# Four algebraic changes to a four-layer graph network on one core: one gate sum for two gates, layer 3 as P + adj²R, the softmax division inside a norm, layer 1's diagonal multiplied in when a transpose is copied out

## The chip, the cores and the metric

The kernel runs on one core of a Trainium2 chip. The metric is the device time of one execution in microseconds (us). All arithmetic is fp32. The runs of one kernel agree within 0.3%.

The engines are named as in the profile: PE is TensorE (matmul), PEld its weight load, DVE is VectorE, ACT is ScalarE, POOL is GpSimd.

## The reference, cut to what matters

The input x has 64 samples of 256 tokens with 128 features, adj is 256x256. Each of the four layers is `x = layernorm(x + layer(x))`. Cuts are marked `...`.

```python
# layer 0, five steps
m  = einsum('nm,bmd->bnd', adj, h)              # m_in == m_out, so av = [m, m]
u3 = h @ u3_w.T + u3_b
z  = sigmoid(av @ w3_w.T + w3_b + u3)
r  = sigmoid(av @ w4_w.T + w4_b + u3)           # the same u3 in both gates
hv = tanh(av @ w5_w.T + w5_b + (r * h @ u5_w.T + u5_b))
h  = (1 - z) * h + z * hv
# layer 1: A is a softmax over edges, built from adj and e alone
out = (A * I) @ (x @ W0) + (A * (1 - I)) @ (x @ W1) + bias
# layer 2
h = x @ Wp + bp
scores = leaky(s_src[:, :, None] + s_dst[:, None, :])      # slope 0.2
scores = where(adj <= 0, lowest, scores)
attn   = softmax(scores)
h_gat  = relu(layernorm((attn * adj) @ h) * gat_g + gat_b)
h_gin  = (1 + eps) * h_gat + adj @ h_gat
z      = relu(layernorm(h_gin @ W1 + b1) * mlp_g + mlp_b)
out    = relu(z @ W2 + b2 + h_gat)
# layer 3: both adjacency inputs are adj
out = x V0 + adj x (V1+V4) + adj^2 x (V2+V5) + adj^3 x (V3+V6)
```

## The kernel before, in the parts that matter

A pair is two samples, that is four tiles of 128 tokens; there are 32 pairs. Layer 0 treats four pairs together, in eight groups of five steps (40 steps), with features on partitions.

```python
# layer 0, one step of a group of four pairs
for i, p in enumerate(pairs):                   # adj times h: four 256-column matmuls into one bank per pair
    ...
for i, p in enumerate(pairs):
    for g, store in ((1, r), (0, z)):
        t = ps()                                # a PSUM bank, 8 in all
        nc.tensor.matmul(t, mat("u3"), hT[p], start=True, stop=False)
        nc.tensor.matmul(t, w345[:, g, :], mT[p], start=False, stop=True)
        ...
        nc.scalar.activation(store[p], t, AF.Sigmoid, bias=bzrh[:, g:g + 1])
    nc.vector.tensor_mul(r[p], r[p], hT[p])
for i, p in enumerate(pairs):                   # candidate hv and new h: two matmuls, tanh, three VectorE operations
    ...
for i, p in enumerate(pairs):                   # h back to tokens on partitions
    t = ps()
    for c in range(4):
        nc.tensor.transpose(t[:, c * P:(c + 1) * P], hT[p][:, c * P:(c + 1) * P], ident)
    ...                                         # VectorE copies it out

# a norm: VectorE, then POOL, then VectorE again
for t in range(4): nc.vector.bn_stats(st[:, t, :], y[:, t, :])
for t in range(4): nc.vector.bn_aggr(mv[:, t, :], st[:, t, :])
nc.gpsimd.tensor_scalar(rs, mv[:, :, 1], LN_EPS, None, op0=ALU.add)
nc.gpsimd.tensor_tensor(rs, rs, neg_half, op=ALU.pow)
for t in range(4): nc.vector.tensor_scalar(o[:, t, :], y[:, t, :], mv[...], rs[...], ...)

# layer 2, attention (l2_scores), its norm's gain and bias (l2_gat)
for c in range(4): nc.vector.scalar_tensor_tensor(u[:, c, :], sd[...], h[:, c, D:D + 1], maskb[...], ...)
nc.vector.scalar_tensor_tensor(l, u, 0.2, u, op0=ALU.mult, op1=ALU.max)         # leaky
nc.vector.tensor_reduce(nm, l, AX.X, ALU.max, negate=True)
for c in range(4): nc.scalar.activation(u[:, c, :], l[:, c, :], AF.Exp, bias=nm[...], accum_out=rd[...])
nc.vector.reciprocal(rd, rd)
for c in range(4): nc.vector.scalar_tensor_tensor(l[:, c, :], u[...], rd[...], a[...], op0=mult, op1=mult)
...
nc.gpsimd.tensor_mul(hg, hg, row("gat_g", 4))
nc.gpsimd.tensor_add(hg, hg, row("gat_b", 4))
nc.vector.tensor_scalar(hg, hg, 0.0, None, op0=ALU.max)                         # "the relu" below
nc.gpsimd.tensor_add(hb, hg, row("b2", 4))                                      # "hb" below

# layers 1 to 3: one stage of each of twelve pairs per tick
stages = [l1_mix, l1_out, l2_xT, l2_scores, l2_wT, l2_gat, l2_gin, l2_z, l2_zT, l2_out, l3_powers, l3_out]
for tick in range(NPAIR + len(stages) - 1):
    for s in reversed(range(len(stages))):
        if 0 <= tick - s < NPAIR:
            stages[s](tick - s)
```

Of the kernel before, what the change touches and what calls it, by code (L numbers as in the profile page):

```python
# [7 lines left out]
F32 = mybir.dt.float32  # L8
# [22 lines left out]
def kernel(ctx: ExitStack, tc: tile.TileContext, x, adj, adjT, mats, cols, rows, out):  # L31
# [60 lines left out]

    w345 = const.tile([P, 3, D], F32, name="w345")
    for i, w in enumerate(("w3", "w4", "w5")):
        nc.vector.tensor_add(w345[:, i, :], mat(w + "a"), mat(w + "b"))
    bzrh = const.tile([P, 3], F32, name="bzrh")
    nc.vector.tensor_add(bzrh[:, 0:1], col("w3_b"), col("u3_b"))
    nc.vector.tensor_add(bzrh[:, 1:2], col("w4_b"), col("u3_b"))
    nc.vector.tensor_add(bzrh[:, 2:3], col("w5_b"), col("u5_b"))

# [1 line left out]
    def ln_stats(y):  # L102
        st = small.tile([P, 4, 6], F32, tag="st", name="st")
        mv = small.tile([P, 4, 2], F32, tag="mv", name="mv")
        for t in range(4):
            nc.vector.bn_stats(st[:, t, :], y[:, t, :])  # L106
        for t in range(4):
            nc.vector.bn_aggr(mv[:, t, :], st[:, t, :])  # L108
        rs = small.tile([P, 4], F32, tag="rs", name="rs")
        nc.gpsimd.tensor_scalar(rs, mv[:, :, 1], LN_EPS, None, op0=ALU.add)  # L110
        nc.gpsimd.tensor_tensor(rs, rs, neg_half, op=ALU.pow)  # L111
        return mv, rs
# [14 lines left out]
    def layer0(pairs):  # L127
# [8 lines left out]
        for s in range(STEPS):  # L136
            for i, p in enumerate(pairs):
                t = ps()
                for b in range(2):
                    for j in range(2):  # L140
                        nc.tensor.matmul(t[:, b * N:(b + 1) * N], h[p][:, 2 * b + j, :], aT[:, j, :],  # L141
                                         start=(j == 0), stop=(j == 1))
                mT[p] = gates.tile([P, 2 * N], F32, tag=f"mT{i}", name="mT", bufs=1)
                nc.scalar.copy(mT[p], t)  # L144
            for i, p in enumerate(pairs):
                for g, store in ((1, r), (0, z)):
                    t = ps()
                    nc.tensor.matmul(t, mat("u3"), hT[p], start=True, stop=False)  # L148
                    nc.tensor.matmul(t, w345[:, g, :], mT[p], start=False, stop=True)  # L149
                    store[p] = gates.tile([P, 2 * N], F32, tag=f"g{g}{i}", name="gate", bufs=1)  # L150
                    nc.scalar.activation(store[p], t, AF.Sigmoid, bias=bzrh[:, g:g + 1])  # L151
                nc.vector.tensor_mul(r[p], r[p], hT[p])  # L152
            hv = {}
            for i, p in enumerate(pairs):
                t = ps()
                nc.tensor.matmul(t, w345[:, 2, :], mT[p], start=True, stop=False)  # L156
                nc.tensor.matmul(t, mat("u5"), r[p], start=False, stop=True)  # L157
                hv[p] = gates.tile([P, 2 * N], F32, tag=f"hv{i}", name="hv", bufs=1)
                nc.scalar.activation(hv[p], t, AF.Tanh, bias=bzrh[:, 2:3])  # L159
                nc.vector.tensor_sub(hv[p], hv[p], hT[p])  # L160
                nc.vector.tensor_mul(hv[p], hv[p], z[p])  # L161
                new = gates.tile([P, 2 * N], F32, tag=f"hT{i}", name="hT")
                nc.vector.tensor_add(new, hT[p], hv[p])  # L163
                hT[p] = new
            for i, p in enumerate(pairs):
                t = ps()
                for c in range(4):
                    nc.tensor.transpose(t[:, c * P:(c + 1) * P], hT[p][:, c * P:(c + 1) * P], ident)  # L168
                if s < STEPS - 1:
                    h[p] = gates.tile([P, 4, D], F32, tag=f"htok{i}", name="h", bufs=1)  # L170
                    nc.vector.tensor_copy(h[p], as_tiles(t))
                else:
                    y = gates.tile([P, 4, D], F32, tag="y", name="y", bufs=3)
                    nc.vector.tensor_add(y, as_tiles(t), x_sb[p])
                    layer_norm(y, x_sb[p])
# [28 lines left out]
    # the number of each edge, -1 elsewhere; rowk marks the row that edge k lies in  # L204
# [32 lines left out]
    # from edge 255 on, the index stops at the last entry  # L237
# [11 lines left out]
    dg = const.tile([P, 2, P], F32, name="dg")  # L249
    for it in range(2):  # L250
# [3 lines left out]
        nc.vector.tensor_sub(blk, blk, dg[:, it, :])  # L254
    offT = const.tile([P, 2, N], F32, name="offT")
# [37 lines left out]
    pw = const.tile([P, 2, 3, N], F32, name="pw")  # L293
    nc.vector.tensor_copy(pw[:, :, 0, :], aT)
    for k in (1, 2):
        t = ps()
        for jt in range(2):
            for kt in range(2):
                nc.tensor.matmul(t[:, jt * N:(jt + 1) * N], a[:, kt, jt * P:(jt + 1) * P], pw[:, kt, k - 1, :],
                                 start=(kt == 0), stop=(kt == 1))  # L300
        nc.vector.tensor_copy(pw[:, :, k, :], t.rearrange("p (t i) -> p t i", i=N))
    v = const.tile([P, 3, D], F32, name="v")
    for k in range(3):
        nc.vector.tensor_add(v[:, k, :], mat(f"v{k + 1}"), mat(f"v{k + 4}"))
# [7 lines left out]
    live = {}  # L312

    def l1_mix(p):
# [6 lines left out]
        for c in range(4):  # L321
            nc.tensor.matmul(d[:, c * P:(c + 1) * P], xs[:, c, :], dg[:, c % 2, :], start=True, stop=True)
# [3 lines left out]
        nc.scalar.copy(dT, d)  # L326
# [23 lines left out]
    def l2_scores(p):  # L350
# [14 lines left out]
        l = work.tile([P, 4, N], F32, tag="l", name="l")  # L365
        for c in range(4):
            b, it = divmod(c, 2)
            nc.vector.scalar_tensor_tensor(u[:, c, :], sd[:, b * N:(b + 1) * N], h[:, c, D:D + 1], maskb[:, it, :],
                                           op0=ALU.add, op1=ALU.add)
        nc.vector.scalar_tensor_tensor(l, u, 0.2, u, op0=ALU.mult, op1=ALU.max)  # L370
        nm = small.tile([P, 4], F32, tag="nm", name="nm")
        nc.vector.tensor_reduce(nm, l, AX.X, ALU.max, negate=True)
        rd = small.tile([P, 4], F32, tag="rd", name="rd")
        for c in range(4):
            nc.scalar.activation(u[:, c, :], l[:, c, :], AF.Exp, bias=nm[:, c:c + 1], accum_out=rd[:, c:c + 1])
        nc.vector.reciprocal(rd, rd)
        for c in range(4):
            nc.vector.scalar_tensor_tensor(l[:, c, :], u[:, c, :], rd[:, c:c + 1], a[:, c % 2, :],  # L378
                                           op0=ALU.mult, op1=ALU.mult)
        live["w", p] = l  # L380
        live["h", p] = h

    def l2_wT(p):
        w = live.pop(("w", p))
        wT = work.tile([P, 2, 2, N], F32, tag="wT", name="wT")
        for b in range(2):
# [5 lines left out]
            nc.scalar.copy(wT[:, b], t.rearrange("p (t i) -> p t i", i=N))  # L392
        live["wT", p] = wT

    def l2_gat(p):
# [8 lines left out]
        mv, rs = ln_stats(tt)  # L404
# [53 lines left out]
    def l3_powers(p):  # L458
        xk = work.tile([P, 2, 4, N], F32, tag="xk", name="xk")
        for b in range(2):  # L460
            lo, hi = ps(), ps()
            xs = [x_sb[p][:, 2 * b + j, :] for j in range(2)]
            for j in range(2):
                nc.tensor.transpose(lo[:, j * P:(j + 1) * P], xs[j], ident)
            for j in range(2):
                nc.tensor.matmul(lo[:, N:], xs[j], pw[:, j, 0, :], start=(j == 0), stop=(j == 1))
            for j in range(2):
                nc.tensor.matmul(hi, xs[j], pw[:, j, 1:3, :].rearrange("p k i -> p (k i)"),  # L468
                                 start=(j == 0), stop=(j == 1))
            nc.scalar.copy(xk[:, b, 0:2, :], lo.rearrange("p (k i) -> p k i", i=N))  # L470
            nc.vector.tensor_copy(xk[:, b, 2:4, :], hi.rearrange("p (k i) -> p k i", i=N))  # L471
        live["xk", p] = xk

    def l3_out(p):
        xk = live.pop(("xk", p))
        t = ps()
        for c in range(4):
            b, i = divmod(c, 2)
            for k in range(4):
                nc.tensor.matmul(t[:, c * D:(c + 1) * D], xk[:, b, k, i * P:(i + 1) * P],  # L480
                                 v[:, k - 1, :] if k else mat("v0"), start=(k == 0), stop=(k == 3))
        y = work.tile([P, 4, D], F32, tag="y", name="y", bufs=3)
        nc.vector.tensor_add(y, as_tiles(t), x_sb[p])
# [4 lines left out]
    stages = [l1_mix, l1_out, l2_xT, l2_scores, l2_wT, l2_gat, l2_gin, l2_z, l2_zT, l2_out, l3_powers, l3_out]  # L488
# [44 lines left out]
```

## Time and profile before

| | before |
|---|---|
| time, median of 4 runs | 2407.32 us (2406.32 to 2408.09) |
| span of the profiled execution | 2405.4 us |
| layer 0 and preparation, to the first matmul of layer 1's mix | 1435.3 us |
| layers 1 to 3, from there | 970.1 us |
| one step of layer 0 (40 of them) | 34.07 us |
| one full tick of layers 1 to 3 | 29.56 us |

The page of a profile gives sums and averages over the span. How the kernel is bound can only be read from a stage of its own: one step of layer 0, and one tick. A timeline line has its start, its length, the engine, the source line, the operation, the tiles, and in brackets the engine's idle time before it and what ended it.

The prediction shows the lines for the bound. Two more of the same tick of before matter later: what POOL and VectorE did to each other around the relu, in the timeline of all engines.

```profile
1861.52 1.27 POOL L328 TENSOR_TENSOR xb<-x,rbc 128x512 f32<-128x512 f32 x1
...
1861.60 1.47 DVE L412 TENSOR_SCALAR hg<-hg 128x512 f32<-128x512 f32 x1 [1.77 <-POOL hg L411]
...
1862.99 1.21 DVE L370 SCALAR_TENSOR_TENSOR l<-u 128x1024 f32<-128x1024 f32 x1
...
1863.15 2.18 POOL L414 TENSOR_TENSOR hb<-hg,rbc 128x512 f32<-128x512 f32 x1 [0.36 <-DVE hg L412]
```

The relu began just after a POOL sum (xb, which is x plus layer 1's bias) and took 1.47 us, where its best is 0.41. Then the roles change: VectorE began the leaky operation, whose inputs are both in SBUF, and the POOL sum that came just after it took 2.18 us in place of 1.27. Whoever comes second waits.

### The profile page before, as it was taken

To read this page: it belongs to the slowest core of one execution; us is meant where nothing else is said; L and a number is where in the kernel's file an instruction comes from. 1 tells how busy PE (TensorE), PEld (TensorE's weight loads), DVE (VectorE), ACT (ScalarE), POOL (GpSimd) and SP (SyncE) were. 2 spreads that over 40 slices of the span, in tenths; PEclk is the share of its full clock that TensorE was granted. 3 is DMA by queue.
4 is the path that set the end of the run, shared out by engine and by line. 5 is a ranking of instruction groups with operands and counts; after the bars stand their busy time and mean duration, and the time that the engine had idled before them with its cause. 6 is when DMAs were issued, how large, how long until landed. Compare 5 with 4: busy or idle time off the path is not lost.

```text
span 2405.4 us, 24775 instructions
## 1 busy us (share of the span) xinstructions
PE 2072.7 (86%) x8820; PEld 1407.6 (59%) x8820; DVE 1327.4 (55%) x3770; ACT 700.5 (29%) x1321; POOL 431.2 (18%) x519
## 2 busy tenths in 40 slices
PE   7996999998998998998999996888888888888887
PEld 4554555554555555555555555776666667666665
DVE  3435444335345335435444446777777777777766
ACT  2331333223322332332233323332222222222221
POOL 0000000000000000000000003444444444443342
PEclk9997999999999999999999998999999999999999
DMA  6000000000000000000000000000000000000000
GB/s 178 1 1 0 0 1 0 1 0 0 1 0 0 1 0 1 1 0 1 0 1 0 0 1 1 1 5 10 9 10 9 10 10 10 10 10 9 14 13 24
DMA packets 35035, 20.66 MB, mean 9 GB/s; under 512 B 1248, under 2 KB 34528, under 8 KB 34912
## 3 DMA queue, kind: packets, MB, share of 16 engines
q1 hardware_dynamic: 34064, 17.04, 2.7%
q10 hardware_dynamic: 848, 2.04, 0.2%
q8 instruction: 70, 1.15, 0.2%
q14 instruction: 53, 0.43, 0.1%
HBM read 10.69 MB, written 8.39 MB: 8 GB/s over the span
## 4 chain that ended last, share of the span: by engine, by line
PE 41%; DVE 40%; POOL 13%; issue 3%; ACT 3%; DMA 0%; POOLq 0%; ACTq 0%; DVEq 0%
PE ps L148 11%; PE ps L149 11%; PE ps L141 11%; POOL rs L111 8%; DVE st L106 5%; DVE hv L161 5%; DVE hv L160 4%; DVE hT L163 4%; DVE x L117 4%; DVE mv L108 2%; DVE l L378 2%; POOL hg L411 2%; POOL rs L110 2%; POOL hg L410 2%; DVE hg L412 2%
## 5 line engine op out<-in xcount | busy, mean ns | idle before, releaser
L152 DVE TENSOR_TENSOR gate<-gate,hT 128x512 f32<-128x512 f32 x160 | 110.8, 692 | 656.5 <-ACT gate L151 656.5
L110 POOL TENSOR_SCALAR rs<-mv 128x4 f32<-128x4 f32 x192 | 44.0, 229 | 1855.3 <-DVE mv L108 1853.0
L148 PE MATMUL ps<-hT,W 128*128 128x512 f32 x640 | 327.2, 593 | 9.8 <-DVE hT L134 9.8
L149 PE MATMUL ps<-mT,w 128*128 128x512 f32 x640 | 326.8, 592 | 0.0
L151 ACT ACTIVATE gate<-ps,bzrh 128x512 f32<-128x512 f32 x320 | 219.8, 687 | 342.0 <-PE ps L149 342.0
L141 PE MATMUL ps<-aT,h 128*128 128x256 f32 x1024 | 266.2, 425 | 0.0
L141 PEld LDWEIGHTS ps<-aT,h 128*128 128x128 f32 x1024 | 223.4, 222 | 36.5
L144 ACT COPY mT<-ps 128x512 f32<-128x512 f32 x160 | 93.6, 585 | 461.9 <-PE ps L141 461.9
L149 PEld LDWEIGHTS ps<-mT,w 128*128 128x128 f32 x640 | 121.6, 190 | 153.1 <-issue 153.1
L148 PEld LDWEIGHTS ps<-hT,W 128*128 128x128 f32 x640 | 121.1, 190 | 147.7 <-issue 102.1
L168 PE MATMUL ps<-ident,hT 128*128 128x128 f32 x640 | 107.6, 309 | 111.3 <-DVE hT L163 111.3
L111 POOL TENSOR_TENSOR rs<-rs,neg_half 128x4 f32<-128x4 f32 x192 | 199.2, 1038 | 15.9
L160 DVE TENSOR_TENSOR hv<-hv,hT 128x512 f32<-128x512 f32 x160 | 109.7, 686 | 109.6 <-ACT hv L159 109.6
L117 DVE TENSOR_SCALAR x<-y,mv,rs 128x128 f32<-128x128 f32 x384 | 109.5, 347 | 108.5 <-POOL rs L111 108.5
L168 PEld LDWEIGHTS ps<-ident,hT 128*128 128x128 f32 x640 | 80.5, 155 | 149.1 <-issue 149.1
L157 PE MATMUL ps<-gate,W 128*128 128x512 f32 x320 | 163.4, 592 | 0.0
L156 PE MATMUL ps<-mT,w 128*128 128x512 f32 x320 | 163.4, 592 | 0.0
L159 ACT ACTIVATE hv<-ps,bzrh 128x512 f32<-128x512 f32 x160 | 110.0, 687 | 162.8 <-PE ps L157 162.8
L409 ACT ACTIVATE hg<-ps,nmr,rs 128x128 f32<-128x128 f32 x128 | 48.1, 456 | 306.5 <-DVE nmr L406 306.5
L480 PE MATMUL ps<-v,xk 128*128 128x128 f32 x768 | 121.2, 300 | 1.5 <-DVE xk L471 1.5
L468 PE MATMUL ps<-pw,x 128*128 128x512 f32 x256 | 120.8, 594 | 1.5 <-DVE h L359 1.5
L106 DVE BATCH_NORM_STATS2 st<-y 128x6 f32<-128x128 f32 x512 | 112.8, 278 | 1.3
(157 smaller groups left out, 3169.0 us busy)
## 6 DMA issues: line engine op xcount, KB each, us to landing
x<-x_in SPq DMA_DIRECT2D x32, 256.0 KB, 5.5
y_out<-o SPq DMA_DIRECT2D x32, 256.0 KB, 2.3
W<-mats_in ACTq DMA_DIRECT2D x1, 832.0 KB, 7.4
W<-mats_in ACTq DMA_DIRECT2D x1, 512.0 KB, 4.4
rbc<-rows_in ACTq DMA_DIRECT2D x1, 385.0 KB, 6.6
aT<-adjT_in SPq DMA_DIRECT2D x1, 256.0 KB, 4.6
a<-adj_in ACTq DMA_DIRECT2D x1, 256.0 KB, 6.0
ccol<-cols_in ACTq DMA_DIRECT2D x1, 6.0 KB, 4.9
```

The source lines that it names most:

```text
L106: nc.vector.bn_stats(st[:, t, :], y[:, t, :])
L111: nc.gpsimd.tensor_tensor(rs, rs, neg_half, op=ALU.pow)
L117: nc.vector.tensor_scalar(o[:, t, :], y[:, t, :], mv[:, t, 0:1], rs[:, t:t + 1], op0=ALU.subtract, op1=ALU.mult)
L141: nc.tensor.matmul(t[:, b * N:(b + 1) * N], h[p][:, 2 * b + j, :], aT[:, j, :], start=(j == 0), stop=(j == 1))
L148: nc.tensor.matmul(t, mat("u3"), hT[p], start=True, stop=False)
L149: nc.tensor.matmul(t, w345[:, g, :], mT[p], start=False, stop=True)
L151: nc.scalar.activation(store[p], t, AF.Sigmoid, bias=bzrh[:, g:g + 1])
L156: nc.tensor.matmul(t, w345[:, 2, :], mT[p], start=True, stop=False)
L157: nc.tensor.matmul(t, mat("u5"), r[p], start=False, stop=True)
L160: nc.vector.tensor_sub(hv[p], hv[p], hT[p])
L168: nc.tensor.transpose(t[:, c * P:(c + 1) * P], hT[p][:, c * P:(c + 1) * P], ident)
L480: nc.tensor.matmul(t[:, c * D:(c + 1) * D], xk[:, b, k, i * P:(i + 1) * P], v[:, k - 1, :] if k else mat("v0"), start=(k == 0), stop=(k == 3))
```

## The change

The intent is to take work off the engine that is the bound in each part.

1. *One gate sum.* `u3·h` is multiplied once per pair and step. The bank first holds `u3·h + w4·m`, ScalarE reads r from it, then `(w3 − w4)·m` is added to the same bank and ScalarE reads z. Sigmoid becomes `(1 + tanh(v/2))/2`, so that ScalarE's program has no sigmoid left.
2. *Layer 3* is `P + adj²R` with `P = x(V0+I) + adj x(V1+V4)` and `R = x(V2+V5) + adj x(V3+V6)`. P waits in PSUM for a tick until `adj²R` is added.
3. *Softmax.* The rows are not divided by their sum den. The norm that follows divides it away if its epsilon becomes `eps·den²`. adj is multiplied in at the evacuation of the transposed weights (wT), on VectorE. ScalarE takes over the leaky function.
4. *Layer 1's diagonal* is no longer a matmul with a diagonal matrix, but a transpose whose evacuation multiplies by the diagonal (dT).

The core of the diff (comments, loads of constants and untouched lines cut):

```diff
+    nc.vector.tensor_sub(w345[:, 0, :], w345[:, 0, :], w345[:, 1, :])
...
             for i, p in enumerate(pairs):
-                for g, store in ((1, r), (0, z)):
-                    t = ps()
-                    nc.tensor.matmul(t, mat("u3"), hT[p], start=True, stop=False)
-                    nc.tensor.matmul(t, w345[:, g, :], mT[p], start=False, stop=True)
-                    ...
-                    nc.scalar.activation(store[p], t, AF.Sigmoid, bias=bzrh[:, g:g + 1])
-                nc.vector.tensor_mul(r[p], r[p], hT[p])
+                gate[p] = ps()
+                nc.tensor.matmul(gate[p], mat("u3"), hT[p], start=True, stop=False)
+                nc.tensor.matmul(gate[p], w345[:, 1, :], mT[p], start=False, stop=True)
+                ...
+                nc.scalar.activation(r[p], gate[p], AF.Tanh, bias=bzrh[:, 1:2], scale=0.5)
+                nc.vector.scalar_tensor_tensor(r[p], r[p], 1.0, hT[p], op0=ALU.add, op1=ALU.mult)
+            for i, p in enumerate(pairs):
+                nc.tensor.matmul(gate[p], w345[:, 0, :], mT[p], start=False, stop=True, skip_group_check=True)
+                ...
+                nc.scalar.activation(z[p], gate[p], AF.Tanh, bias=bzrh[:, 0:1], scale=0.5)
...
         for c in range(4):
-            nc.tensor.matmul(d[:, c * P:(c + 1) * P], xs[:, c, :], dg[:, c % 2, :], start=True, stop=True)
+            nc.tensor.transpose(d[:, c * P:(c + 1) * P], xs[:, c, :], ident)
-        nc.scalar.copy(dT, d)
+        nc.vector.tensor_mul(dT..., d..., drow[:, None, :].to_broadcast([P, 2, N]))
...
-        for c in range(4):
-            nc.vector.scalar_tensor_tensor(u[:, c, :], sd[...], h[:, c, D:D + 1], maskb[:, it, :], ...)
-        nc.vector.scalar_tensor_tensor(l, u, 0.2, u, op0=ALU.mult, op1=ALU.max)
-        nc.vector.tensor_reduce(nm, l, AX.X, ALU.max, negate=True)
-        ... exp, reciprocal, four products with rd and a
+        for b in range(2):
+            nc.vector.tensor_add(u[:, 2 * b:2 * b + 2, :], sd[...].to_broadcast([P, 2, N]), maskb)
+        nc.vector.tensor_reduce(nm, u, AX.X, ALU.max)
+        nc.vector.tensor_add(nm, nm, ss)
+        nc.vector.tensor_scalar(nm2, nm, -1.0, None, op0=ALU.mult)
+        nc.vector.scalar_tensor_tensor(nm, nm, -0.2, nm2, op0=ALU.mult, op1=ALU.min)
+        for c in range(4):
+            nc.scalar.activation(l[:, c, :], u[:, c, :], AF.Prelu, bias=ss[:, c:c + 1], alpha=0.2)
+        for c in range(4):
+            nc.scalar.activation(u[:, c, :], l[:, c, :], AF.Exp, bias=nm[:, c:c + 1], accum_out=den[:, c:c + 1])
...
-            nc.scalar.copy(wT[:, b], t.rearrange("p (t i) -> p t i", i=N))
+            nc.vector.tensor_mul(wT[:, b], t.rearrange("p (t i) -> p t i", i=N), aT)
...
-    def l3_powers(p): ...   # x, adj x, adj^2 x, adj^3 x, copied out by ScalarE and VectorE
-    def l3_out(p): ...      # sixteen products with the weights, y = sum + x on VectorE
+    def l3_q(p): ...        # x^T and (adj x)^T
+    def l3_mix(p): ...      # P and R into two banks, R copied out by VectorE in two halves (rr)
+    def l3_out(p): ...      # adj^2 R added into P's banks, y copied out by ScalarE
```

## The prediction

> **What bounds the kernel now.** I first read the page's strip of busy tenths, because the kernel has two parts that look different. Each digit is a fortieth of the span, some 60 us.
>
> ```profile
> PE   7996999998998998998999996888888888888887
> PEld 4554555554555555555555555776666667666665
> DVE  3435444335345335435444446777777777777766
> ...
> PEclk9997999999999999999999998999999999999999
> ```
>
> Up to slice 24 TensorE is full and VectorE is at 0.3 to 0.5: this is layer 0. From there PE drops to 0.8 and VectorE rises to 0.7: layers 1 to 3. The TensorE timeline puts the border at 1435 us (the first matmul of layer 1's mix), so layer 0 with the preparation takes 1435 us and the rest 970 us.
>
> Layer 0 by its groups (after the first bar busy us and mean ns; after the second the engine's idle time before, and who ended it):
>
> ```profile
> L148 PE MATMUL ps<-hT,W 128*128 128x512 f32 x640 | 327.2, 593 | 9.8 <-DVE hT L134 9.8
> L149 PE MATMUL ps<-mT,w 128*128 128x512 f32 x640 | 326.8, 592 | 0.0
> L168 PE MATMUL ps<-ident,hT 128*128 128x128 f32 x640 | 107.6, 309 | 111.3 <-DVE hT L163 111.3
> ```
>
> Gate matmuls wait for nothing; only the transposes wait (111 us over 40 steps, 2.8 us each) for VectorE's new h. One matmul of the program is two instructions. The timeline inside a step starts two of them every 0.86 us (a mean of 593 ns hides that they overlap), so a 512-column matmul costs PE 0.857 us. The chain of waits has the steps' adj products start at 49.82, 83.88, 117.95 and 152.02 us: 34.07 us a step. By parts: 8.2 adj products, 16 x 0.857 = 13.7 gates, 8 x 0.857 = 6.9 candidate, 5.2 transposes with waits: 34.0. **Layer 0 is bound by PE, gap-free except at the transposes.**
>
> Layers 1 to 3 run one stage of each of many pairs per tick. L378 comes back at 1839.53 and 1869.10 us: 29.57 us a tick. VectorE over that tick (last bracket: its idle time and who ended it):
>
> ```profile
> 1844.47 1.11 DVE L117 TENSOR_SCALAR o<-y,mv,rs 128x128 f32<-128x128 f32 x4 [0.90 <-POOL rs L111]
> ...
> 1850.64 1.11 DVE L117 TENSOR_SCALAR x<-y,mv,rs 128x128 f32<-128x128 f32 x4 [1.10 <-POOL rs L111]
> ...
> 1853.90 1.11 DVE L117 TENSOR_SCALAR z<-z,mv,rs 128x128 f32<-128x128 f32 x4 [1.09 <-POOL rs L111]
> ...
> 1857.16 0.16 DVE L406 SCALAR_TENSOR_TENSOR nmr<-mv,rs 128x4 f32<-128x4 f32 x1 [1.16 <-POOL rs L111]
> ...
> 1861.60 1.47 DVE L412 TENSOR_SCALAR hg<-hg 128x512 f32<-128x512 f32 x1 [1.77 <-POOL hg L411]
> ...
> 1867.87 1.11 DVE L117 TENSOR_SCALAR x<-y,mv,rs 128x128 f32<-128x128 f32 x4 [1.48 <-POOL rs L111]
> ```
>
> These six are all its gaps: 7.5 us. They are round trips to POOL inside the norms, and VectorE never waits for PE here. The other 22.06 us it works. PE's matmuls, added up by their steps in the same tick (0.107 us a transpose, 0.22, 0.43 and 0.857 us for 128, 256 and 512 columns), need only 22.4 us of it, and its gaps end mostly on VectorE. **Layers 1 to 3 are bound by VectorE's stream plus its POOL round trips.**
>
> **What the Trainium skill says.** (1) "SBUF — State Buffer", Who interferes with whom: VectorE in a 2-port mode (tensor_scalar and copy can enter it) and GpSimd lock each other out for a whole instruction. The trace agrees: L412 takes 414 ns at its best and 1473 at the median; in the tick above POOL's L328 starts at 1861.52, just before L412 at 1861.60, and ends at 1862.79, 0.28 us before L412 does. (2) "VectorE: DVE Perf Modes", Why PSUM operands drop a tier: an fp32 operation with a PSUM operand runs at 1x. Agrees: 512 columns from PSUM take 0.66 to 0.69 us, the same for add, copy or the three-operand form, so exchanging these forms in layer 0 is free. (3) "ScalarE: Activation LUTs", Table sets: tanh lies in exp's set, and each switch is a load. The trace has five loads of 1.28 us; in the changed program's order one is left, also with Prelu. (4) "TensorE: Matmul & The Clock Gate", Part 1: after an idle window of 3.4 us the clock is halved. Agrees: after the transposes' waits the granted clock reads 0.50 from 1401 to 1404 us, and adj products take 8.1 to 8.2 us in place of 6.9.
>
> **The change, part by part.**
>
> *One gate sum.* Per pair and step u3·h is multiplied once in place of twice: 4 pairs x 0.857 = 3.43 us of PE per step, 40 steps: **-137 us**. The new wait: the z product must not enter the bank until ScalarE has read r. The program's order has four (u3, r) pairs first, then four z products. r of the last pair is summed at 8 x 0.857 = 6.9 us and read by 7.9; its z product comes at 6.9 + 3 x 0.857 = 9.4. The first z product at 6.9 needs a read done by 2.6. Both covered. The halved tanh forms keep the instruction counts on ScalarE (687 ns both) and VectorE, and VectorE's order in the candidate part stays, so the transposes' 2.8 us and the cold window stay. New step: 34.07 - 3.43 = 30.64.
>
> *Preparation.* adj^3 goes: of the two rounds at 216.0 to 222.2 us one falls away with its copy, two small matmuls come: about **-4 us**.
>
> *VectorE per pair in layers 1 to 3*, by issue-to-issue times in the tick above. Removed: four score sums L368 1.57, leaky L370 1.14, reciprocal 0.21, L378 1.63, two xk copies 1.27, the y add 0.72: 6.54. Added (by like instructions): dT product 0.61, two u sums 1.22, two wT products 1.22, two 256-column copies 0.70, four tiny ones 0.45: 4.20. Net -2.3. Besides, in the new order POOL does hb and then xb after the relu, so none of its work is in flight at the relu, which should run in 0.42: -1.0. Together -3.3.
>
> *POOL round trips.* Each is 1.56 us from the last aggregate to the next use, less what the order puts between. In the new order this is, in turn: two statistics (0.40), one rr copy (0.35), two statistics, two statistics, one wT product (0.61): gaps of 1.16, 1.21, 1.16, 1.16, 0.95. The relu waits for the chain nmr, ScalarE, two POOL ops: 4.44 us (1857.16 to 1861.60), with 2.6 us put in: 1.83. Sum 7.5, as before. So the tick becomes 22.06 - 3.3 + 7.5 = 26.2 us.
>
> *PE per tick:* layer 3 from 9.28 us to 7.32 (4 transposes 0.43, 4 x 256 columns 1.73, 8 x 256 3.44, 4 x 256 1.72), dg as transposes -0.44: 22.4 to 20.0. That lies beside VectorE and is worth nothing itself. *ScalarE* gains about 1 us a tick (four Prelu, two y halves against the copies moved away), at under 0.3 busy: hidden.
>
> *Sum for layers 1 to 3:* 32 x 3.3 = 106 us less; the last eight ticks have no score stage and are partly bound by PE and latency, so I take 10 off, and one more stage at the end costs about 4: **-95 to -100**.
>
> Total: 2407 - 137 - 4 - 100 = 2166; I say **2165 us**.
>
> **The rivals.** *A: PE becomes the bound of the tick through PSUM slots.* The two layer-3 sums keep two of eight banks for most of a tick, and in the new order PE's transposes of x wait for a bank that VectorE's first wT product frees. Walking PE through the tick, I find it done with its second stretch some 6 us before that, idle; that may halve the clock for 3.4 us (a loss of 1.7). With it the l2 output is summed about 0.7 us before VectorE wants it, without it nearly 4. If that is off by 1 to 2 us, it costs 30 to 60 us: 2195 to 2225. *B: the relu stays at 1.47* because POOL still collides: +32 us, 2197. *C: the gates' bank wait bites*, 0.5 to 1 us in each step: +20 to +40; against it stand the margins above. *D: the cold windows vanish* in layer 0, as the shorter step shifts them: 1.25 us in some 30 steps, -37. Against: 30.64 us is nearly nine windows of 3.41 as 34.07 is nearly ten, so it should stay locked as now. *E: layer 3 or ScalarE's work was the bound*: against it, VectorE's gaps all end on POOL.
>
> **Range and chances.** A or B alone gives about 2200, D 2125. Eight in ten: **2125 to 2210**. PE's removed 137 us in a gap-free part alone is 5.7%, so faster by over 2%: 0.98; same 0.015; slower 0.005.
>
> **What would show it right or wrong.** Right: steps of layer 0 at 30.6 us, z products without idle time before them; a tick of about 26 us; six VectorE gaps on POOL of 7.5 us together; the relu at 0.42 us; the clock below full once in most ticks. Wrong: VectorE waiting for PE in the tick (A), the relu above 1 us (B), PE waiting for ScalarE ahead of the z products (C), adj products at 6.9 us (D).

## The result, and the profile after

| | before | after |
|---|---|---|
| time, median of 4 runs | 2407.32 us | 2174.61 us (2174.32 to 2176.47) |
| layer 0 and preparation | 1435.3 us | 1297.0 us |
| layers 1 to 3 | 970.1 us | 876.1 us |
| one step of layer 0 | 34.07 us | 30.67 us in the first two groups, then 29.4 to 31.5 |
| full tick, mean of 18 ticks | 29.56 us | 26.61 us |

The ratio after to before is 0.9037, with a 95% interval of 0.9024 to 0.905. A ratio is the mean time of one kernel's runs over that of the other's runs of the same rounds, so it is not quite the ratio of the medians.

Busy tenths of the changed kernel in 40 slices of some 54 us:

```profile
PE   7895889888988988898889887878888888888887
...
DVE  3435445445346336435444457776676767677776
...
PEclk9997999999999999999999998988888889898999
```

The border between the parts is still near slice 24. PEclk is new: it is 0.8 in most slices of layers 1 to 3, where it was 0.9 before. PE has less work in a tick, and is granted a lower clock for what is left.

The groups of layer 0's matmuls in the changed kernel (busy us and mean ns; then the idle time before them and what ended it):

```profile
L157 PE MATMUL ps<-hT,W 128*128 128x512 f32 x320 | 164.5, 595 | 13.1 <-DVE hT L143 13.1
L158 PE MATMUL ps<-mT,w 128*128 128x512 f32 x320 | 163.4, 592 | 0.0
...
L163 PE MATMUL ps<-mT,w 128*128 128x512 f32 x320 | 143.8, 592 | 0.0
L181 PE MATMUL ps<-ident,hT 128*128 128x128 f32 x640 | 102.8, 299 | 111.2 <-DVE hT L176 111.2
```

L157 now counts 320 where the u3 products were 640. L163, the z products that share a bank with r, waited for nothing. The transposes wait 111.2 us, as before (111.3).

The steps are not all alike. From the fourth group of pairs on they take 31.5, 29.4 and 30.5 us in turn, and the adj products (L150) of a group's five steps take 7.07, 9.55, 7.07, 8.15 and 8.27 us. In all they take 267.1 us, where those of before (L141) take 266.2.

VectorE in one tick of the changed kernel, the slowest of a cycle of five ticks. nmr is a small operation of layer 2's norm that comes once a tick, and dT is layer 1's diagonal product; the last bracket is its idle time and who ended it. The lines between, which follow one another without a gap, are cut.

```profile
1644.42 1.12 DVE L126 TENSOR_SCALAR x<-y,mv,rs 128x128 f32<-128x128 f32 x4 [1.10 <-POOL rs L120]
...
1647.68 1.11 DVE L126 TENSOR_SCALAR z<-z,mv,rs 128x128 f32<-128x128 f32 x4 [1.09 <-POOL rs L120]
...
1650.87 0.16 DVE L433 SCALAR_TENSOR_TENSOR nmr<-mv,rs 128x4 f32<-128x4 f32 x1 [0.82 <-POOL rs L120]
...
1655.31 0.43 DVE L439 TENSOR_SCALAR hg<-hg 128x512 f32<-128x512 f32 x1 [1.81 <-POOL hg L438]
...
1658.94 0.69 DVE L346 TENSOR_TENSOR dT<-ps,drow 128x512 f32<-128x512 f32 x1 [1.41 <-PE ps L342]
1659.55 0.16 DVE L395 TENSOR_SCALAR nm<-nm 128x4 f32<-128x4 f32 x1
...
1662.30 1.12 DVE L126 TENSOR_SCALAR x<-y,mv,rs 128x128 f32<-128x128 f32 x4 [1.10 <-POOL rs L120]
...
1665.57 1.12 DVE L126 TENSOR_SCALAR o<-y,mv,rs 128x128 f32<-128x128 f32 x4 [1.16 <-POOL rs L120]
```

The six gaps on POOL are there: 1.10 + 1.09 + 0.82 + 1.81 + 1.10 + 1.16 = 7.08 us. The relu is at 0.43. A seventh gap is new: dT waits 1.41 us for PE. Over the whole run the waits view of VectorE gives this wait as 16.1 us in 17 ticks.

What PE did ahead of that, in the same tick, and the granted clock in four stretches of it (start and end, length, then busy us of PE, PEld, DVE, ACT and POOL with their instructions, then PEclk and the DMA's share and GB/s):

```profile
1650.11 0.66 PE L366 MATMUL ps<-ident,x 128*128 128x128 f32 x4 [2.61 <-DVE wT L415]
1651.69 0.79 PE L357 MATMUL ps<-W,qT 128*128 128x128 f32 x2 [0.93 <-DVE wT L415]
...
1655.27 3.20 PE L339 MATMUL ps<-offT,x 128*128 128x256 f32 x8
1658.30 0.60 PE L342 MATMUL ps<-ident,x 128*128 128x128 f32 x4
```

```profile
1651.00:1654.40 3.40, 2.71 (x12) 2.71 (x13) 2.50 (x6) 3.33 (x9) 1.67 (x2) 0.51 0.00 0
1654.40:1657.80 3.40, 3.40 (x12) 2.89 (x11) 2.22 (x4) 0.50 (x2) 2.40 (x3) 0.50 0.00 0
1657.80:1661.20 3.40, 3.40 (x19) 2.99 (x18) 2.26 (x13) 1.98 (x7) 1.23 (x2) 0.98 0.01 2
1647.60:1651.00 3.40, 0.66 (x4) 0.42 (x4) 2.50 (x13) 0.00 (x0) 1.25 (x3) 1.00 0.00 0
```

PE is idle for 2.61 us and then 0.93 us, because a PSUM bank comes free only with VectorE's wT product. In that stretch it is busy for 0.66 of 3.40 us. For the next two stretches the clock reads 0.51 and 0.50, so that layer 1's mix, L339, takes 3.20 us; the eight like matmuls of L450 earlier in the tick took 1.89. dT's transposes, L342, come after it.

The length of a tick follows a cycle of five: from one nmr to the next it is 26.24, 26.26, 26.55, 26.93, 27.11 us, again and again. The dT wait grows with it: 0, 0.33, 0.85, 1.22, 1.41 us. Where it is 0, the small operation L395 takes 0.79 us; where it is 0.33, 0.37 us; in the others 0.16.

The cycle also shows what makes PE late. In every tick PE starts L357 0.82 us after nmr and has the same products to do up to L342. What differs is how much of them falls under the halved clock. Layer 1's mix in the four ticks of a cycle whose dT waits are 0, 0.33, 0.85 and 1.22 us:

```profile
1549.00 1.89 PE L339 MATMUL ps<-offT,x 128*128 128x256 f32 x8
...
1575.53 2.12 PE L339 MATMUL ps<-offT,x 128*128 128x256 f32 x8
...
1601.78 2.64 PE L339 MATMUL ps<-offT,x 128*128 128x256 f32 x8
...
1628.34 3.01 PE L339 MATMUL ps<-offT,x 128*128 128x256 f32 x8
```

In the tick where dT does not wait, the clock is halved for 3.4 us only (it reads 0.50 from 1545.3 to 1548.7 and 1.00 after). In the other four it is halved for 6.8.

### The profile page after: what moved, and what is told of

Its sections match the earlier page's. It is cut to its first block, busy times and chain, and to the rows that moved or that the text cites. A ratio compares the mean times of both kernels' runs of the same rounds, so it can differ in the third digit from the quotient of the medians. Undisturbed runs are those within 1.5% of the kernel's fastest.

```text
span 2173.1 us, 22736 instructions
## 1 busy us (share of the span) xinstructions
PE 1873.2 (86%) x7856; PEld 1329.3 (61%) x7856; DVE 1232.1 (57%) x3709; ACT 723.8 (33%) x1413; POOL 404.2 (19%) x519
## 4 chain that ended last, share of the span: by engine, by line
PE 43%; DVE 38%; POOL 13%; issue 3%; ACT 2%; DMA 1%; POOLq 0%; DVEq 0%
PE ps L150 13%; POOL rs L120 9%; PE ps L163 6%; PE ps L157 6%; PE ps L158 6%; DVE st L112 5%; DVE hv L174 5%; DVE x L126 5%; DVE hv L173 5%; DVE hT L176 5%; DVE mv L114 2%; PE ps L339 2%; PE ps L357 2%; POOL rs L117 2%; DVE o L126 2%
## 5 line engine op out<-in xcount | busy, mean ns | idle before, releaser
L161 DVE SCALAR_TENSOR_TENSOR gate<-gate,hT 128x512 f32<-128x512 f32 x160 | 110.6, 691 | 452.3 <-ACT gate L160 452.3
L117 POOL TENSOR_SCALAR rs<-mv 128x4 f32<-128x4 f32 x160 | 36.5, 228 | 1578.4 <-DVE mv L114 1576.2
L150 PE MATMUL ps<-aT,h 128*128 128x256 f32 x1024 | 267.1, 427 | 0.0
L150 PEld LDWEIGHTS ps<-aT,h 128*128 128x128 f32 x1024 | 222.9, 221 | 36.7
L181 PE MATMUL ps<-ident,hT 128*128 128x128 f32 x640 | 102.8, 299 | 111.2 <-DVE hT L176 111.2
L157 PE MATMUL ps<-hT,W 128*128 128x512 f32 x320 | 164.5, 595 | 13.1 <-DVE hT L143 13.1
L126 DVE TENSOR_SCALAR x<-y,mv,rs 128x128 f32<-128x128 f32 x384 | 108.9, 347 | 98.7 <-POOL rs L120 98.7
L158 PE MATMUL ps<-mT,w 128*128 128x512 f32 x320 | 163.4, 592 | 0.0
L170 PE MATMUL ps<-gate,u5h 128*128 128x512 f32 x320 | 163.4, 592 | 0.0
L169 PE MATMUL ps<-mT,w 128*128 128x512 f32 x320 | 163.4, 592 | 0.0
L163 PE MATMUL ps<-mT,w 128*128 128x512 f32 x320 | 143.8, 592 | 0.0
L174 DVE SCALAR_TENSOR_TENSOR hv<-gate,hv 128x512 f32<-128x512 f32 x160 | 110.3, 689 | 4.1
L176 DVE SCALAR_TENSOR_TENSOR hT<-hv,hT 128x512 f32<-128x512 f32 x160 | 109.8, 686 | 2.7
```

The lines of the kernel that those rows point to most:

```text
L126: nc.vector.tensor_scalar(o[:, t, :], y[:, t, :], mv[:, t, 0:1], rs[:, t:t + 1], op0=ALU.subtract, op1=ALU.mult)
L150: nc.tensor.matmul(t[:, b * N:(b + 1) * N], h[p][:, 2 * b + j, :], aT[:, j, :], start=(j == 0), stop=(j == 1))
L157: nc.tensor.matmul(gate[p], mat("u3"), hT[p], start=True, stop=False)
L158: nc.tensor.matmul(gate[p], w345[:, 1, :], mT[p], start=False, stop=True)
L163: nc.tensor.matmul(gate[p], w345[:, 0, :], mT[p], start=False, stop=True, skip_group_check=True)
L169: nc.tensor.matmul(t, w345[:, 2, :], mT[p], start=True, stop=False)
```

## The experiments

Twelve kernels ran. Each gave the right result, and its ratio is against the kernel before on the same chip.

### The four parts, each alone on the kernel before

**gate_only.** The gate part of the diff and nothing else.

```diff
+                nc.tensor.matmul(gate[p], mat("u3"), hT[p], start=True, stop=False)        # once, for r and z
+                nc.tensor.matmul(gate[p], w345[:, 1, :], mT[p], start=False, stop=True)
...
+                nc.tensor.matmul(gate[p], w345[:, 0, :], mT[p], start=False, stop=True, skip_group_check=True)
```

> Before plus the one gate sum alone. My theory: 3.43 us of PE leave each of 40 gap-free steps, so a step takes 30.6 us in place of 34.07 and the whole 2270 us, with no idle time of PE before the z products. Rival (the z product waits for ScalarE to have read r from the same bank): idle PE before the z products, steps of 31.2 us or more, 2290 us or more.

Measured: 2270.47 us, ratio 0.9434 (0.9418 to 0.9449). That is 136 us less than before in its rounds (2406.43). The tick stays at 29.56. The first step of the prediction holds alone.

**l3_only.** Layer 3's part of the diff, with its preparation.

```diff
-    stages = [..., l3_powers, l3_out]
+    stages = [..., l3_q, l3_mix, l3_out]
```

> Before plus layer 3 as P + adj^2 R alone. My theory: only VectorE's part of it counts (two xk copies 1.27 and the y add 0.72 go, two rr copies 0.70 come: -1.3 us a tick), the 2 us that PE saves a tick count nothing: tick 28.3 us, total about 2366 us. Rival 1 (PE's saving counts): tick 27.5 or less, 2345 us or less. Rival 2 (the two banks held for most of a tick make PE the bound): tick 29.5 or more, VectorE waiting for PE, 2400 us or more.

Measured: 2363.59 us, ratio 0.9826 (0.9812 to 0.9841), tick 28.17 us. VectorE's 1.3 us a tick came off, and 1.39 was gained. PE's saving of 2 us a tick did not show. The record calls this run the same, since it is below 2%, but its interval does not reach 1.

**soft_only.** The softmax part: undivided weights, `eps·den²` in the norm, adj at the evacuation.

```diff
-        ... leaky, reciprocal, l = u * rd * a            # VectorE
+        ... AF.Prelu, AF.Exp with accum_out=den          # ScalarE
-            nc.scalar.copy(wT[:, b], t...)
+            nc.vector.tensor_mul(wT[:, b], t..., aT)
-        mv, rs = ln_stats(tt)
+        mv, rs = ln_stats(tt, d2)                        # d2 = eps * den * den
```

> Before plus the softmax division inside the norm and adj at the transpose's evacuation alone. My theory: VectorE loses 4.55 us and gains 2.9 us a tick, the relu still collides with POOL's xb (1.47 us) in this order, the POOL gaps stay at about 7.6 us: tick 28.0 us, total about 2357 us. Rival (ScalarE's four Prelu are on the path): tick 29 us or more, VectorE or PE waiting for ScalarE, 2390 us or more.

Measured: 2345.53 us, ratio 0.9747 (0.9733 to 0.9762), tick 27.46 us. This part gave 60.9 us, some 11 more than expected: the tick was 0.54 us shorter than the 28.0 expected. Its relu still has a median of 1.475 us, so the relu's gain is not in it. Of the 0.54, POOL gaps account for 0.43 (7.17 us, where 7.6 were expected). The rest was not followed up.

**l1_only.** Layer 1's diagonal as a transpose and a product.

```diff
-            nc.tensor.matmul(d[...], xs[:, c, :], dg[:, c % 2, :], start=True, stop=True)
+            nc.tensor.transpose(d[...], xs[:, c, :], ident)
-        nc.scalar.copy(dT, d)
+        nc.vector.tensor_mul(dT..., d..., drow...)
```

> Before plus the diagonal as a transpose and a product at its evacuation alone. My theory: 0.61 us more of VectorE a tick, but in this order it stands inside a POOL round trip that was 1.48 us of idle time, so nothing changes: 2400 to 2412 us. Rival (work added to VectorE always counts): +0.61 us in 32 ticks, 2427 us. Second rival (PE's 0.44 us a tick saved counts): 2393 us.

Measured: 2408.8 us, ratio 1.0014 (0.9999 to 1.0029). VectorE has 0.65 us more to do in each tick, and it costs next to nothing: in this run's tick dT begins at 1872.42 directly after the statistics of a norm, inside the round trip to POOL. The wait that followed was 0.90 us, where that of before was 1.48.

The sum of the four is −136.0 − 42.8 − 60.9 + 2.4 = −237.3 us; the whole change gave −232.7. In none of layer 3, softmax and diagonal alone did the relu drop below 1.47 us in a full tick: that is an effect of the whole, where POOL does hb and then xb after the relu.

### What the relu's collision with POOL is worth

**pool_dummy.** The changed kernel, with an unused POOL sum that is in flight when the relu starts.

```diff
-        nc.gpsimd.tensor_add(hg, hg, row("gat_b", 4))
+        hr = work.tile([P, 4, D], F32, tag="hr", name="hr")
+        nc.gpsimd.tensor_add(hr, hg, row("gat_b", 4))
+        scr = work.tile([P, 4, D], F32, tag="scr", name="scr")
+        nc.gpsimd.tensor_add(scr, hg, row("b2", 4))
+        hg = hr
```

> After with one unused POOL addition of 512 columns put right behind the addition of gat_b, on a tile that the relu does not touch, so that POOL is at work while the relu runs; VectorE's order is that of after. My theory (the relu needs a port that POOL holds): relu back from 0.43 to 1.47 us, but in the ticks where VectorE waits up to 1.4 us for PE ahead of the dT product, that wait takes most of it up: about 2190 us (2182 to 2198). Rival 1 (no collision, the relu was fast for another cause): relu 0.43 us, 2175 us. Rival 2 (VectorE's work always counts): 31 x 1.05 = +33 us, 2207 us.

Measured: 2202.56 us, ratio 0.9155 (0.9141 to 0.9169), 28 us more than the changed kernel. That is above the theory's 2182 to 2198, and nearer to rival 2's 2207. All its full ticks are 27.32 us.

```profile
1721.20 1.26 POOL L441 TENSOR_TENSOR scr<-hg,rbc 128x512 f32<-128x512 f32 x1
...
1721.27 1.47 DVE L443 TENSOR_SCALAR hr<-hr 128x512 f32<-128x512 f32 x1 [1.83 <-POOL hr L439]
...
1725.06 0.78 DVE L395 TENSOR_SCALAR nm<-nm 128x4 f32<-128x4 f32 x1
```

The relu is back at 1.47, 1.04 us more than in the changed kernel, so rival 1 is out. The tick grew only by 27.32 − 26.61 = 0.71. The wait for PE at dT, 0.76 us in the mean of a cycle, is gone: VectorE comes there later, when PE is done. But without it the small operation L395 takes 0.78 us in every tick, where its mean over a cycle was 0.33. That the expectation had not counted: 1.04 − 0.76 + 0.45 = 0.73. So the relu's term is right in size, and the losses partly hide each other.

### What the half clock in the tick is worth

**warm_tick2** and **warm_tick3.** The changed kernel with the product of the destination scores done two or three times into the same bank, so that PE is busy where it waited.

```diff
-        nc.tensor.matmul(sd, vdst, xT, start=True, stop=True)
+        for _ in range(3):            # warm_tick2: range(2)
+            nc.tensor.matmul(sd, vdst, xT, start=True, stop=True)
```

> After with the score product of 512 columns done twice (same result). It adds 0.86 us of PE ahead of PE's gap, but the scheduler now puts both adj^2 R products behind the gap, so the gap stays as long. My theory: the clock stays halved for some 3 to 7 us a tick, VectorE still waits for PE ahead of dT, 2165 to 2185 us. Rival (more PE work in the tick is what costs): 0.86 us in 20 ticks, 2190 us or more.

> After with the score product done three times (same result): PE's gap ahead of the transposes of x is shorter by 0.86 us; VectorE's order changes in one place, the dT product now stands inside a POOL round trip. My theory (the halved clock after the gap made PE late for dT): the clock reads 1.0 in most ticks, VectorE does not wait for PE, tick 25.8 us, about 2152 us. Rival (PE is late because of its amount of work or of its banks): VectorE's wait for PE stays or grows, 2175 us or more.

Both expectations failed in their times, which lie in the rivals' ranges, but not for the rivals' reasons. warm_tick2 took 2193.1 us (ratio 0.9116), with a clock of 0.87 in the ticks: a product more did not keep the clock up, and the dT wait rose to 25.9 us in 21 ticks. VectorE's order changed too, and one POOL round trip (L126 o) takes 1.47 us where it took 1.16. warm_tick3 took 2182.76 us (ratio 0.9072). It did what it was meant to do: clock 0.95 in the ticks, no wait of dT for PE, and dT now inside a POOL round trip. (At its old place dT would not have waited either: in the tick below its transposes end at 1609.65, and VectorE gets there at 1611.28.) Still its full ticks are mostly 26.45 us, 26.56 in the mean. The timeline shows what came instead:

```profile
1611.29 1.27 POOL L349 TENSOR_TENSOR xb<-x,rbc 128x512 f32<-128x512 f32 x1 [0.46 <-DVE nm L395]
...
1611.45 1.13 DVE L396 TENSOR_SCALAR nm<-nm 128x4 f32<-128x4 f32 x1
```

The small negation of four columns (nm2) took 1.13 us in place of 0.16, in the shadow of POOL's xb. In the changed kernel the wait for PE had mostly kept it until xb was done.

**nm_fix** and **tick3_nm.** I took this for the relu's collision in miniature, that of a tensor_scalar, and removed the tensor_scalar: on the changed kernel (nm_fix) and on warm_tick3 (tick3_nm).

```diff
-        nc.vector.tensor_reduce(nm, u, AX.X, ALU.max)
-        nc.vector.tensor_add(nm, nm, ss)
-        nc.vector.tensor_scalar(nm2, nm, -1.0, None, op0=ALU.mult)
-        nc.vector.scalar_tensor_tensor(nm, nm, -0.2, nm2, op0=ALU.mult, op1=ALU.min)
+        nc.vector.tensor_reduce(nm, u, AX.X, ALU.max, negate=True)
+        nc.vector.scalar_tensor_tensor(nm2, ss, -1.0, nm, op0=ALU.mult, op1=ALU.add)
+        nc.vector.scalar_tensor_tensor(nm, nm2, 0.2, nm2, op0=ALU.mult, op1=ALU.min)
```

> The changed kernel, but the row maximum's negative comes from the reduce itself (negate), so the small 128x4 tensor_scalar goes (one small instruction fewer; its work moves into the three-operand form, which was never seen blocked). In the changed kernel that tensor_scalar takes 0.16 us in three ticks of five, 0.79 and 0.36 us in the other two. Theory (it is slow only when POOL has the 128x512 bias sum in flight, the collision of the relu in miniature): 0.17 us a tick from the collision and 0.15 from the instruction that goes, over some 28 ticks: about 9 us less, 2166. Rival (VectorE was waiting in those ticks for something else and only the wait moves): 2173 to 2176.

> The same edit on the variant with the score product done three times, where the small tensor_scalar takes 1.13 us in every tick and the tick is 26.45 us. Theory: tick 26.45 - 0.98 - 0.15 = 25.3 us, over 26 full ticks and part of the ramp: 2182.8 - 30 = about 2153, with the clock near full in the tick. Rival (PE is then the next bound, at 21.7 us of matmuls a tick and waits of its own): the tick stays above 25.8 us and the time above 2165.

Measured: nm_fix 2172.72 us (ratio 0.9031, 0.9016 to 0.9046), tick3_nm 2181.61 us (0.9067, 0.9053 to 0.908). nm_fix lies just below its rival's 2173 to 2176, far from a clear gain, and tick3_nm is above its rival's 2165. So both theories fell. The rival's reason for tick3_nm, PE as the next bound, is not what the trace shows: VectorE waits for PE's layer 2 output in 8 ticks, 4.9 us in all. In nm_fix the operation at that place, L395, still takes up to 1.13 us and 438 ns in the mean, where the tensor_scalar had 409. In tick3_nm the tick is still 26.4 us:

```profile
1612.27 1.27 POOL L349 TENSOR_TENSOR xb<-x,rbc 128x512 f32<-128x512 f32 x1 [0.46 <-DVE nm L395]
1612.43 1.12 DVE L396 SCALAR_TENSOR_TENSOR nm<-nm 128x4 f32<-128x4 f32 x1
```

Now it is the three-operand form that is blocked, at the same place: 0.16 us after xb's start, and until xb is done, as it was in warm_tick3. What matters is not the form that I blamed, but that an operation of either form falls into xb's time. The Trainium skill has both in "SBUF — State Buffer", Who interferes with whom: besides tensor_scalar, "A DVE instruction with two SBUF inputs contends with a GpSimd instruction that reads SBUF", and the three-operand form here has two. I had read that section for tensor_scalar alone. The lines of the kernel before shown above agree with it too, the other way around: hb took 2.18 us behind the leaky operation. To gain this microsecond xb would have to run at another time, clear of these operations; that was not tried.

### What the waits at layer 0's transposes are worth

**warm_both3.** warm_tick3, and in layer 0 a useless 512-column product ahead of the transposes of the third and fourth pair, which are those that wait.

```diff
                 t = ps()
+                if i >= 2:
+                    nc.tensor.matmul(t, w345[:, 2, :], mT[p], start=True, stop=True)
                 for c in range(4):
                     nc.tensor.transpose(...)
```

> warm_tick3 and, in layer 0, one 512-column product each (overwritten after it) ahead of the transposes of pairs 3 and 4 of a group, where PE waits for VectorE. My theory (the half clock behind that wait costs 1.2 to 1.7 us a step, and the scheduler besides moves one adj product into the wait): adj products at full clock, steps of about 28.7 us, about 2076 us. Rival (the added 1.71 us of PE work costs in full): steps of 32 us, 2220 us.

Measured: 2123.83 us, ratio 0.8828 (0.8815 to 0.8841). The first nmr of layer 2 comes at 1293.3 us in place of warm_tick3's 1350.6: 57 us from layer 0, less than the 76 that the expectations imply (2152 − 2076). A step within a group of four pairs is 28.44 us; the transposes wait 3.2 us in all, but a new wait of the adj products for their input h (20.4 us) took some of it. Useless work made the kernel faster, since it fell into idle time and kept the clock up. So the question was whether useful work can go there.

**early2.** The changed kernel, nothing added: the *next* step's `u3·h` of the first two pairs is done there.

```diff
+        gate = {}
         for s in range(STEPS):
...
-                gate[p] = ps()
-                nc.tensor.matmul(gate[p], mat("u3"), hT[p], start=True, stop=False)
+                if p not in gate:
+                    gate[p] = ps()
+                    nc.tensor.matmul(gate[p], mat("u3"), hT[p], start=True, stop=False)
...
-                nc.scalar.activation(z[p], gate[p], AF.Tanh, ...)
+                nc.scalar.activation(z[p], gate.pop(p), AF.Tanh, ...)
...                                     # ahead of the transposes of pair i:
+                if s < STEPS - 1:
+                    for q in {2: (0,), 3: (1,)}.get(i, ()):
+                        gate[pairs[q]] = ps()
+                        nc.tensor.matmul(gate[pairs[q]], mat("u3"), hT[pairs[q]], start=True, stop=False)
```

> The changed kernel with layer 0 reordered, nothing added: the next step's products of h for the first two pairs of a group are done ahead of the transposes of the third and of the fourth pair, where PE waited 2.8 us. Four steps of five have it (32 of 40). Theory (the wait can be filled, and a filled wait keeps the clock up): each such step loses 1.72 us of wait, and about 1.4 us of half clock as the filled variant before showed (30.66 to 28.43 us with 1.72 us of useless work): about 3.1 x 32 = 100 us less, 2075. Rival (the banks held by the early sums make PE wait elsewhere, or the clock still halves): only the 1.72 or less per step, 2120 or more.

Measured: 2074.88 us (2074.05 to 2074.98), ratio 0.8623 (0.861 to 0.8636), as the theory had it. A step within a group is 27.27 us in place of the 30.67 of the first groups. One step of early2 by PE:

```profile
95.70 1.02 PE L183 MATMUL ps<-hT,W 128*128 128x512 f32 x2
97.48 0.63 PE L186 MATMUL ps<-ident,hT 128*128 128x128 f32 x4 [0.75 <-DVE hT L177]
97.94 1.02 PE L183 MATMUL ps<-hT,W 128*128 128x512 f32 x2
99.28 0.63 PE L186 MATMUL ps<-ident,hT 128*128 128x128 f32 x4 [0.31 <-DVE hT L177]
99.74 7.07 PE L151 MATMUL ps<-aT,h 128*128 128x256 f32 x32
```

and of the changed kernel:

```profile
102.33 0.63 PE L181 MATMUL ps<-ident,hT 128*128 128x128 f32 x4 [1.60 <-DVE hT L176]
104.13 0.63 PE L181 MATMUL ps<-ident,hT 128*128 128x128 f32 x4 [1.17 <-DVE hT L176]
104.59 8.76 PE L150 MATMUL ps<-aT,h 128*128 128x256 f32 x32
```

The waits fall from 2.77 to 1.06 us, that is 1.71 by the two products moved into them. The adj products fall from 8.76 to 7.07, that is 1.69, by the clock alone: it reads 1.00 from 99 to 107 us in early2, and 0.82 from 104 to 113.5 us in the changed kernel. Together 3.40, the difference of the two steps. Four steps of five have the early products. In the whole run the transposes' waits fall from 111.2 to 56.4 us and the adj products from 267.1 to 226.3: 54.8 us of waits and 40.8 us of clock, 95.6 of the 99.7 us gained.

**best3.** Three early products per step (two ahead of the third pair, one ahead of the fourth), with the edits of tick3_nm.

> All together: three products of h moved into the transposes' waits in layer 0 (two ahead of the third pair's transposes, one ahead of the fourth's), the score product three times and no small tensor_scalar in the tick. Theory: layer 0 some 100 to 110 us less than the changed kernel, the ticks 22 less: about 2045 to 2055, clock 0.97 or above. Rival (three sums held early starve the adj products of banks): layer 0 no better than in the variant with useless fill, 2100.

Measured: 2050.2 us (2046.98 to 2052.57), ratio 0.852 (0.8505 to 0.8534). The step is 26.41 us. All of the gain on the changed kernel is layer 0: the first nmr comes 126 us earlier (1221.9 against 1348.2), and from the first to the last nmr it takes 762.3 us against 761.3. The edits in the tick gave nothing here either. So the total lies within the theory's 2045 to 2055 by luck: layer 0 gave more than the 100 to 110 expected, the ticks nothing in place of 22, and the clock was 0.962, below 0.97. This is the fastest kernel.

## Why the prediction was right, and where it was off

The time predicted was 2165 us, the time measured 2174.61, inside the range. Point by point:

- **One gate sum, −137 us: right.** −136 alone, and in the whole −138.3 with the preparation, for −141 predicted. The bank wait (rival C) did not come. The cold windows of layer 0 cost as much as before (267.1 us of adj products for 266.2), so rival D did not come in the sum. But the steps did not stay locked, as the prediction argued: 14 of 40 have their adj products at or near full clock, where 8 had before, and others take up to 9.6 us.
- **PE's 2.4 us a tick are worth nothing: right, and even less than nothing.** l3_only gained VectorE's share alone. In the whole change the idle PE lost its clock.
- **VectorE's sum and the POOL gaps: right mechanism, a little too small a gain.** A tick without its dT wait and without the slow small operation would be some 25.7 us, an estimate from the lines above (27.11 − 1.41; 26.93 − 1.22; 26.24 − 0.63), where 26.2 was predicted. The six gaps are 7.08 us, not 7.5, and the work is 18.63 us, not 18.8. soft_only shows the same surplus.
- **The relu: right.** 0.43 us in 31 of 32 ticks, and pool_dummy shows its price.
- **Rival A is the term that was mis-sized.** The prediction had PE idle in the tick, one cold window of 3.4 us, a loss of 1.7 us, and "With it the l2 output is summed about 0.7 us before VectorE wants it". The runs show two cold windows in four ticks of five, and VectorE's wait not at the l2 output but earlier, at the diagonal product: 16.1 us in 17 ticks. Mean 26.61 − 25.7 = 0.9 us a tick is lost by that wait and by the collision that shows where the wait is short.
- **The sum of layers 1 to 3:** −94 for −95 to −100. The prediction's own terms, 106 − 10 − 4, come to −92 and not to −95 to −100, and its total took −100. The surplus of 0.5 us a tick and the loss of 0.9 partly cancel, so that the total came nearer than its parts is in part luck.
- **Two readings beside the sum.** It called the exchange of VectorE's forms in layer 0 free because of operations that read PSUM. The exchanged ones have their operands in SBUF; the exchange was free all the same (L152 692 ns before, L161 691 after). And it took the clock of 0.50 in layer 0 as agreement with an idle window of 3.4 us, though the waits there are 1.6 us and less; the list at the end comes back to this.

The sign named for rival A, VectorE waiting for PE in the tick, did appear. warm_tick3 shows that removing it does not bring its 0.9 us back, since the small operation then runs into POOL's xb. What the tick would gain with both gone was not shown.

The five-tick cycle fits windows of fixed length: 133.1 us for five ticks is 39 windows of 3.413 us, the length that the Trainium skill gives in "TensorE: Matmul & The Clock Gate", Part 1. The clock record of the traces has the same grid: in all 14 runs, every change of the clock lies on one grid of 3.413 us. And runs with other ticks fit it too. nm_fix repeats after four ticks of together 105.8 us, 31 windows; pool_dummy and warm_tick2 have ticks of 27.3 us, 8 windows, which are all alike.

## What to carry to other kernels

Look at what an engine does in its short waits: PE's clock was halved after waits of 1.6 us and less, and useful matmuls moved into those waits gave 100 to 126 us, nearly as much as removing 137 us of matmuls did. After one wait is removed, look at what now starts earlier and whom it meets: here a wait for PE had been keeping a small VectorE operation out of POOL's way. Read the costs of a tick from its own timeline and try each part alone; an estimate that hits the total can hide two errors that cancel.

## What the Trainium skill lacked or had wrong

- "TensorE: Matmul & The Clock Gate", Part 1, says that the clock halves after an idle window and is full again after a busy one, but not how much idleness makes a window idle or busy. The traces show it. Count PE's busy time, as the profile has it, in each window of 3.413 us in all 14 runs (the first 15 us left out). From full clock, the clock was halved after 801 windows, with PE busy for at most 1.69 us in 799 of them (1.92 in two), and stayed full after windows of 1.41 us or more. From half clock, it came back after windows of 2.70 us or more, and stayed halved after windows of 2.95 us or less, but for two. So gaps of 1.60 + 1.17 us between transposes halved it for the adj products (8.76 us), and gaps of 0.75 + 0.31 us with matmuls between did not (7.07 us). In the tick, a stretch of 3.40 us with 0.66 us of PE work halved it, and a stretch with 2.71 us of work did not bring it back; the next one, full of work, did.
- Part 4 of the same page says that transposes don't count as busy in the same way. Here, in fp32, they do: in nm_fix, PE has only transposes from 825.87 to 829.28 us, at half clock, is busy for 3.40 of 3.41 us with them, and the clock is full in the next window.
- The same page's advice with a number is about gaps above 3.4 us. That shorter idles between groups of matmuls can do it, it tells of one kernel ("A second HAM failure mode"), without a size. No single gap at layer 0's transposes is above 1.6 us, and the clock still fell: keeping it up by filling them was worth 1.69 us in the step shown, and 40.8 us in the run.
- "SBUF — State Buffer", Who interferes with whom, was right, and more complete than my reading of it. It gives no size for small operations: one of 128x4 elements, 0.16 us alone, took 1.13 us as a tensor_scalar and 1.12 us in the three-operand form beside a POOL sum of 1.27 us.
- No page has the cost of POOL's power of 128x4 elements, 1.03 us on average over 192 of them, as the profile's rough POOL spans have it. It stands in each of the six round trips that bound a tick.
